# A decoder layer and a gated cross attention: first sums and normalizations in another order, MLP weight pieces over more steps, softmax reciprocal ahead of the smallest values

## The chip, the cores and the metric

The kernel runs on one core of one Trainium2 chip, as one program. The metric is the device time of one execution in microseconds (us). The engines are TensorE (PE; its weight loads are listed apart as PEld), VectorE (DVE), ScalarE (ACT), GpSimd (POOL) and SyncE (SP, which issues most DMAs). Each runs its own instructions in order and waits on semaphores for the others.

## The reference

Everything is float32: `x` is 16 batches of 128 tokens by 512 features, the context `ctx` likewise. There are 16 heads of 32 features.

```python
def layer0(x, ctx):                                 # decoder layer
    ln = layernorm(x, ln1_s, ln1_b)
    q, k, v = split(ln @ w_qkv + b_qkv, 3)
    x = x + merge(attention(q, k, v, mask_SxS)) @ w_ao + b_ao
    ln = layernorm(x, ln2_s, ln2_b)
    q = ln @ w_q + b_q;  k, v = split(ctx @ w_kv + b_kv, 2)
    x = x + merge(attention(q, k, v, mask_BxSxS)) @ w_co + b_co
    ln = layernorm(x, ln3_s, ln3_b)
    return x + gelu(ln @ w1 + b1) @ w2 + b2         # 512 -> 2048 -> 512

def layer1(x, ctx):                                 # gated cross attention
    a = layernorm(ctx, gamma, beta)
    q, k, v = x @ Wq.T, a @ Wk.T, a @ Wv.T
    return x + tanh(gate) * (merge(attention(q, k, v, mask_BxS)) @ Wo.T)

out = layer1(layer0(x, ctx), ctx)
# attention: softmax(q k^T / sqrt(32) * mask - 10000 * (1 - mask)) v, by head
```

## The kernel before

The 16 batches are handled in four groups of four batches (512 tokens). The stages follow each other: self attention of groups A0 to A3, cross attention of B0 to B3, the MLP of the four groups (C0 to C3), and the gated cross attention of D0 to D3. Tiles carry these letters in their names (`s_A`, `ln_C`, `k_D`; a digit for the group is left out in the profile). The token activations `x` stay in SBUF.

The order on each engine is the order in which the program is written down (`keep_in_program_order`). `attend` writes it in steps: a group has 16 steps, four for each batch, and a step handles one unit, which is the scores of a batch for four heads (a 128x512 tile). Unit k goes through the steps as follows: in its own step DVE multiplies the scores out of PSUM by the mask's factor (`scale_unit`) and POOL adds the mask's second term (`add_mask`; the gated stages D have no such addition on POOL); a step later DVE finds each row's smallest value (`least_unit`; the scores are kept with the sign turned, so this is the softmax's maximum) and ACT takes four exponentials with row sums (`exp_unit`); two steps later DVE takes the reciprocal of the sums and POOL multiplies by it (`norm_unit`); three steps later DVE transposes 32x32 squares and SP writes the unit to DRAM (`turn_unit`, tile `away`). SP reads two units back in turned order (`receive_pair`, tile `pT`), PE multiplies by the values (`mix`, tile `av`), and PE multiplies by the output weight (`out_project`, tile `mo`).

Beside the units, each step runs the jobs of the next group (`jobs`: its q, k and v products and what belongs to them) and prepares the group after that (`prepare`: normalizations, which go to DRAM as `turned` and come back as `back`). What must wait for a PE result is put off with `afterwards` and written down when `due()` is called, at a step's start.

The q, k and v products of stage A, and the MLP's products, use block products: a 512x512x512 product becomes seven products of blocks instead of eight, with sums of weight blocks (`left_blocks`, tiles `sums`, made once) and of token blocks (`right_blocks`, tiles `sums_A`, made for each group) before them, and sums out of PSUM after them. One block product is eight matmuls of 128x256. `BLOCKS` gives the steps at which the seven products are issued. Products 1, 6 and 7 add up in one PSUM bank (`mm0`), and ACT copies the bank after each; products 5 and 3 share `mm1`; products 2 and 4 use one of the two banks `pt`.

Before the first group there are no units to run beside. `SelfAttention.begin` normalizes A0 (`normalize`: DVE's statistics, POOL's power for the inverse deviation, then the normalization itself), transposes it on PE, and makes the sums of the q weights; `attend` then runs the jobs of A0 in 16 steps and prepares A1 beside them. In `normalize`, a flat tile is normalized by DVE (`rest`), a tile in squares (all groups after the first) by ACT with an offset from DVE (`rest_in_squares`).

The gated layer's weights must be turned: `gated_weight` loads a weight in 32x32 squares (16 DMAs), DVE transposes it in four parts, and each part is kept in DRAM. In the kernel before this happens to Wk beside the first products, to Wv beside A0's attention (in the jobs of A1), to Wq and Wo in stage B.

The MLP starts beside the last group of stage B. `beside_last_cross` gives its jobs by step, from 0 to 23: key and value products of D0 (`gated_start`), the normalization of C0 (`mlp_start`, whose four reads back, `back_C`, come at step 6), and `piece`, which runs the generator `mlp` on by one `yield`. The first weights `w1_0`, `w1_1` and `w2_0` (1 MB each) are loaded in four pieces each, one piece per `next`:

```python
        while pieces:
            pieces.popleft()()
            yield
```

`piece` calls `due()` first, so that in steps 2 to 13 deferred work is also written down inside the step.

Of the kernel before, what the change touches and what calls it, by code (L numbers as in the profile page):

```python
# [16 lines left out]
P = 128  # L17
# [4 lines left out]
H = 512  # L22
# [30 lines left out]
def decoder_then_gated_cross_attention(ctx: ExitStack, tc: tile.TileContext, a: dict, out: bass.AP):  # L53
# [7 lines left out]


    flip, in_blocks = [0], [True]

    def ps(tag, name):
        if tag == "mm" and in_blocks[0]:
# [151 lines left out]
    def normalize(src, dst, name, then):  # L218

        mv = work.tile([P, 2], F32, tag="mv", name=f"mv_{name}", bufs=4)  # L220
        st = work.tile([P, 6], F32, tag="st", name=f"st_{name}", bufs=4)
        nc.vector.bn_stats(st, src)
        nc.vector.bn_aggr(mv, st)
        rstd = work.tile([P, 1], F32, tag="rstd", name=f"rstd_{name}", bufs=4)
        nc.vector.tensor_scalar(rstd, mv[:, 1:2], EPS, None, ALU.add)
        nc.gpsimd.tensor_tensor(rstd, rstd, mhalf[:, 0:1], ALU.pow)

        def rest():
            nc.vector.tensor_scalar(dst, src, mv[:, 0:1], rstd, ALU.subtract, ALU.mult)
            then()  # L230

        def rest_in_squares():

            off = work.tile([P, 1], F32, tag="off", name=f"off_{name}", bufs=4)
            nc.vector.scalar_tensor_tensor(off, mv[:, 0:1], -1.0, rstd, ALU.mult, ALU.mult)
            nc.scalar.activation(by_chunk(dst), squares(src), AF.Identity, bias=off, scale=rstd)
            afterwards("dve", then)

        afterwards("dve", rest if len(dst.shape) == 2 else rest_in_squares)

    def ln_tile(name):
        return work.tile([P, GB, NQ, KC, Q], F32, tag="ln", name=f"ln_{name}")
# [322 lines left out]
    def attend(sections, ready, others, after=None):  # L565

        if not ready:
            sections[0].begin()
            jobs = sections[0].jobs()
            for p in range(NS):
                due()
                for job in jobs.get(p, ()):
                    job()
                sections[1].prepare(p)
        units, batches = [], []
        projected = deque()  # L580

        def step(k, bt=None, jobs=(), ahead=None, last=True):

            m = k % GB
            pair = k - 5
            if pair % 2 and 0 <= pair < len(units):
                receive_pair(*units[pair])
            if m == 0 and bt is not None:
                scores(bt)
            due()  # L590
            for job in jobs:
                job()
# [12 lines left out]
            if 0 <= k - 3 < len(units):  # L605
                turn_unit(*units[k - 3])
            if 0 <= k - 1 < len(units):
                least_unit(*units[k - 1])
                exp_unit(*units[k - 1])
            if 0 <= k - 2 < len(units):  # L610
                norm_unit(*units[k - 2])
            if bt is not None:
                for j in SCALED[m]:
                    scale_unit(bt, j)
                bt.sec.add_mask(by_head(bt.s[m]), bt.b)

# [29 lines left out]
    class SelfAttention(Section):  # L646
# [16 lines left out]
            elif p >= 12:  # L663
                group_back(self.lnT, self.back, "ln1_s", "ln1_b", [p - 12])

        def begin(self):

            ln = work.tile([P, GB, H], F32, tag="ln", name="ln_A0")
            self.lnT = act_tile("A0")
            tp = []  # L670
            for b in range(GB + 1):
                if b == 1:
                    turn_vectors(0)
                    tp += [ps("sc", f"tp_A0_{k}") for k in range(KC)]
                left = late["dve"].popleft() if b else None
                if b < GB:
                    normalize(x[0][:, b, :], ln[:, b, :], f"A0_{b}", lambda b=b: transpose_batch(tp, ln, b))
                if left is not None:
                    left()
            transposed_out(self.lnT, tp, "ln1_s", "ln1_b")  # L680

            at_ = [wpool.tile([P, GB, 2, HF], F32, tag="w", name=f"sums_{n}") for n in range(2)]
            masks = [work.tile([P, 2, 2, HF], F32, tag="mask", name=f"sums_A{n}", bufs=2) for n in range(2)]
            at_ = [t[:, n] for t in at_ for n in range(GB)] + [masks[1][:, 1]]
            SelfAttention.tokens_at = [masks[0][:, 0], masks[0][:, 1], masks[1][:, 0]]
            SelfAttention.weights = []
            for n, key in enumerate(("sq", "sk", "sv")):
                sides, todo = left_blocks(w[key], at_[3 * n : 3 * n + 3])  # L690
                SelfAttention.weights.append(sides)
                SelfAttention.weight_sums.append(todo)
            for o in SelfAttention.weight_sums[0]:
                nc.vector.tensor_tensor(*o)

        weight_sums = []
        v_bias = "b_qkv", 2 * KC

        def jobs(self):
            g, n, lnT = self.g, self.name, self.lnT  # L700
            qkv_tiles(self)
            sides, todo = right_blocks(lnT, self.tokens_at)
            sums = [lambda o=o: nc.gpsimd.tensor_tensor(*o) for o in todo], [0, 0, 1, 2]
            v = self.v
            products = [
                block_product(halves(self.q), self.weights[0], sides, False, f"q_{n}", ("b_qkv", 0)),
# [7 lines left out]
            if g == 0:  # L714
                others = [o for todo in self.weight_sums[1:] for o in todo]
                rows = [lambda b=b: add_row(0, bo_row, b) for b in range(GB)]
                more = (
                    *small_jobs(), *gated_weight("k", "enc", 7), ([lambda o=o: nc.vector.tensor_tensor(*o) for o in others], [1, 2, 3, 3, 4, 5, 6, 7]),
                    (rows, range(8, 12)),
                )  # L720
            elif g == 1:
                more = ([lambda b=b: load_batch(3, b) for b in range(GB)], [1, 3, 5, 7]), *gated_weight("v", "enc")
            return plan(sums, *blocks_plan(products), *more)

        def scale_mask(self, s, sc, b):
# [25 lines left out]
    class CrossAttention(Section):  # L751
# [32 lines left out]
        def jobs(self):  # L784
# [9 lines left out]
            out += [lambda c=c: project_chunk(self.k, w["ck"], encT, c, f"k_{n}", "b_k", 0) for c in range(KC)]  # L794
            out += [lambda b=b: values_chunk(self.v, w["cv"], encT, b, f"v_{n}", w["bcv"]) for b in range(GB)]
            return plan(
                (out, PRODUCTS), ([lambda: mask_terms(self.ms, self.ma)], [7]), *(gated_weight("qo"[g - 1]) if g in (1, 2) else ()),
                *((late_weights(),) if g == 0 else ())
            )

# [34 lines left out]

    def mlp_start(ml):


        ml.b2 = load_row(a["L0_xattn_b2"], "b2_row")
        ml.db1 = cpool.tile([P, NF], F32, tag="db1", name="db1")  # L840
# [31 lines left out]
    def mlp(ml, last_steps):  # L872
# [12 lines left out]

        kept, unkept, pieces = {}, [], deque()

        def load(n, which):  # L890
            g, i = steps[n]
# [125 lines left out]
        w1, w2, right1, right2 = {}, {}, {}, {}  # L1017

        w1[0], w1[1], w2[0] = load(0, 1), load(1, 1), load(0, 2)
        while pieces:  # L1020
            pieces.popleft()()
            yield

        right1[0], todo, _ = sums(0, 1, "kT", w1.pop(0), nc.gpsimd)
        for do in todo:
# [87 lines left out]
    def gated_weight(key, tag="w", first=0):  # L1113

        t = []

        def begin(c, half):
            if not t:
                t.append(act_tile(f"gw_{key}", "enc") if tag == "enc" else wpool.tile([P, KC, H], F32, tag="w", name=f"gw_{key}"))
            load_turned(t[0], a[f"L1_xattn_W{key}"], c, (2 * half, 2 * half + 1))  # L1120

        def turn(c):
# [1 line left out]
            afterwards("act", lambda: keep_part(f"g{key}", t[0], c))  # L1124

        return (
            ([lambda c=c, half=half: begin(c, half) for c in range(KC) for half in range(2)], range(first, first + 8)),
            ([lambda c=c: turn(c) for c in range(KC)], [8, 10, 12, 14] if first == 0 else [12, 13, 14, 15]),
        )

    class FirstGated:
# [130 lines left out]
    def beside_last_cross():  # L1262
# [2 lines left out]
            due()  # L1265
            next(in_mlp)

        at_ = [*range(2, 14), 8, 10, 12, 14, 15, 15, 16, 16, 17, 18, 19, 19, 20, 21, 21, 22, 23, 23]
        pieces = [piece] * len(at_)
        return plan(*gated_start(first), *mlp_start(ml), (pieces, at_))  # L1270

    def beside_last_gated():
        return plan((deferred, [1, 3, 5, 7, 9, 11, 16, 17, 19]))
# [72 lines left out]
```

## Time and profile before

| | |
|---|---|
| time, median of 3 runs | 1218.19 us (1218.03 to 1218.56) |
| the profiled execution's own time | 1217.82 us |
| span from first to last instruction | 1215.8 us |
| mean granted TensorE clock | 0.989 |
| busy, share of the span: PE | 1170.9 us, 96% |
| DVE | 749.1 us, 62% |
| POOL | 592.1 us, 49% |
| ACT | 585.1 us, 48% |
| HBM | 158.70 MB read, 89.13 MB written, 204 GB/s |
| first scores of A0 on PE | 62.10 us from the span's start |

In a timeline line stand the start and the duration in us, engine, line and operation, then the tiles as written<-read, the shapes and the count; in brackets the idle time of the engine before it and what ended that. Almost every instruction is recorded through one helper, so the line is L49 throughout and the tiles tell them apart. "issue" means that the profile shows no releaser. SPq and ACTq are DMA issues on those queues.

### The profile page before, as it was taken

Reading aid. Unit: us, or ns where it says so; the run is one execution under the profiler, and the core shown is the slowest. Engines: PE = TensorE matmul, PEld = TensorE weight load, DVE = VectorE, ACT = ScalarE, POOL = GpSimd, SP = SyncE. Lnnn points to the kernel's source line nnn. Section 1 sums busy time; section 2 is a strip of 40 time slices with the busy share of each in tenths; the row PEclk is TensorE's granted clock in tenths of the full one; section 3 lists DMA queues with packets and bytes.
Section 4 is the critical chain, followed back from the end, with each engine's and each line's share of the span. In section 5 each row is a group of like instructions: output and inputs, shape, how many; then the busy total and the mean of one; then the engine's idle time right before and its main releaser. Section 6 shows DMA issues by size and latency. Waiting matters only on the chain.

```text
span 1215.8 us, 20222 instructions
## 1 busy us (share of the span) xinstructions
PE 1170.9 (96%) x6707; PEld 775.3 (64%) x6707; DVE 749.1 (62%) x1452; ACT 585.1 (48%) x2042; POOL 592.1 (49%) x547
## 2 busy tenths in 40 slices
PE   5979999999999999988999999999999999999997
PEld 4767777744444444434688888888888754444443
DVE  6587979786777767774755443552432247557673
ACT  2256676766665565565222232232222246768652
POOL 4377868675767665567224433443341133323331
PEclk8999999999999999999999999999999999999999
DMA  5768477898887977797694484486447628676575
GB/s 201 181 168 235 144 195 192 226 258 231 194 229 186 235 215 221 191 254 222 201 352 168 170 296 171 156 250 252 148 160 262 194 81 225 167 211 182 166 226 181
DMA packets 317983, 249.18 MB, mean 205 GB/s; under 512 B 82932, under 2 KB 278200, under 8 KB 313016
## 3 DMA queue, kind: packets, MB, share of 16 engines
q1 hardware_dynamic: 317840, 247.89, 69.4%
q8 instruction: 53, 0.87, 0.3%
q14 instruction: 50, 0.41, 0.1%
q10 hardware_dynamic: 40, 0.01, 0.0%
HBM read 158.70 MB, written 89.13 MB: 204 GB/s over the span
## 4 chain that ended last, share of the span: by engine, by line
PE 74%; POOL 9%; issue 6%; DVE 6%; DMA 3%; ACT 1%; SPq 1%; ACTq 0%; POOLq 0%
PE o L49 14%; PE h L49 14%; PE mm_q_D L49 5%; PE mm_v_B L49 5%; PE mm_k_B L49 5%; PE mm_q_B L49 5%; PE mo_A L49 4%; PE mm_v_D L49 4%; PE mm_k_D L49 3%; PE mo_B L49 3%; PE mm_v_A L49 3%; POOL s_A L49 3%; PE mm_k_A L49 2%; PE mo_D L49 2%; POOL s_B L49 2%
## 5 line engine op out<-in xcount | busy, mean ns | idle before, releaser
L49 POOL TENSOR_TENSOR s_D<-s_D,sum_D 128x512 f32<-128x512 f32 x64 | 66.5, 1039 | 142.7 <-DVE sum_D L49 135.3
L49 ACT ACTIVATE s_B<-s_B,mn_B 128x128 f32<-128x128 f32 x256 | 99.5, 390 | 73.9 <-issue 50.9
L49 DVE TENSOR_TENSOR h<-h,h 128x512 f32<-128x512 f32 x80 | 54.9, 686 | 119.1 <-PE h L49 118.7
L49 ACT ACTIVATE s_A<-s_A,mn_A 128x128 f32<-128x128 f32 x256 | 99.6, 393 | 58.4 <-issue 34.3
L49 ACT ACTIVATE s_D<-s_D,mn_D 128x128 f32<-128x128 f32 x256 | 99.4, 390 | 40.1 <-issue 33.3
L49 ACT ACTIVATE h<-h 128x512 f32<-128x512 f32 x64 | 40.3, 630 | 157.9 <-DVE h L49 153.7
L49 POOL TENSOR_TENSOR s_B<-s_B,sum_B 128x512 f32<-128x512 f32 x64 | 67.3, 1052 | 76.9 <-DVE sum_B L49 66.2
L49 POOL TENSOR_TENSOR s_A<-s_A,sum_A 128x512 f32<-128x512 f32 x64 | 66.6, 1040 | 62.6 <-DVE sum_A L49 60.0
L49 POOL TENSOR_TENSOR s_B<-s_B,mask 128x512 f32<-128x512 f32 x64 | 82.3, 1285 | 0.5 <-DVE s_B L49 0.5
L49 POOL TENSOR_TENSOR s_A<-s_A,ma 128x512 f32<-128x512 f32 x64 | 81.6, 1275 | 0.2 <-DVE s_A L49 0.2
L49 POOL TENSOR_TENSOR sh<-h 128x512 f32<-128x512 f32 x32 | 41.5, 1296 | 53.0 <-ACT h L49 43.3
L49 POOL TENSOR_TENSOR rstd_aD<-rstd_aD,mhalf 128x1 f32<-128x1 f32 x12 | 6.6, 550 | 115.2 <-DVE rstd_aD L49 101.8
L49 PE MATMUL h<-T_C,w 128*128 128x256 f32 x256 | 61.1, 381 | 1.1 <-DVE h L49 1.0
L49 PE MATMUL h<-sx,t 128*128 128x256 f32 x256 | 60.7, 380 | 1.2 <-POOL sx L49 1.2
L49 DVE STREAM_TRANSPOSE s_D<-s_D 128x512 f32<-128x512 f32 x64 | 45.4, 709 | 26.3 <-POOL s_D L49 26.2
L49 PE MATMUL h<-T_C,t 128*128 128x256 f32 x256 | 60.7, 380 | 0.6 <-DVE h L49 0.5
L49 PE MATMUL mo_B<-w_co,mT_B 128*128 128x512 f32 x128 | 59.0, 604 | 2.0 <-ACT mT_B L49 2.0
L49 PE MATMUL mo_D<-w_go,mT_D 128*128 128x512 f32 x128 | 57.9, 601 | 2.8 <-ACT mT_D L49 2.8
L49 PE MATMUL mo_A<-w_ao,mT_A 128*128 128x512 f32 x128 | 59.2, 605 | 1.4 <-ACT mT_A L49 1.4
L49 PE MATMUL o<-w,h 128*128 128x256 f32 x256 | 60.5, 379 | 0.0
L49 PE MATMUL o<-t,h 128*128 128x256 f32 x256 | 60.5, 379 | 0.0
L49 PE MATMUL o<-t,sh 128*128 128x256 f32 x256 | 60.5, 379 | 0.0
(216 smaller groups left out, 2770.9 us busy)
## 6 DMA issues: line engine op xcount, KB each, us to landing
t<-kept SPq DMA_DIRECT2D x24, 1024.0 KB
away_A<-s_A SPq DMA_DIRECT2D x64, 256.0 KB
pT_A<-away_A SPq DMA_DIRECT2D x128, 128.0 KB
away_B<-s_B SPq DMA_DIRECT2D x64, 256.0 KB
pT_B<-away_B SPq DMA_DIRECT2D x128, 128.0 KB
away_D<-s_D SPq DMA_DIRECT2D x64, 256.0 KB
pT_D<-away_D SPq DMA_DIRECT2D x128, 128.0 KB
w<-in_L_xattn_w_dram SPq DMA_DIRECT2D x24, 512.0 KB
```

The lines of the kernel that those rows point to most:

```text
L49: return lambda *args, **kw: self.tc.keep_in_program_order(call(*args, **kw))
```

## The change

It has five parts.

1. Until the first attention steps begin, a tile in squares is normalized by DVE, too (`at_start`). From then on ACT does it, as before.
2. The four sums of the q weights move from DVE to POOL. The four token sums of A0 move from POOL to DVE, and all four are written down at once. The preparation of A1 starts one step sooner: its first batch's statistics stand ahead of A0's last step into `T_A`.
3. The turning of Wk gets a tile of its own (one of the two `v` buffers), with loads at steps 4 to 11 instead of 7 to 14. The turning of Wv moves from the jobs of A1 to those of A2, that is from beside A0 to beside A1.
4. In each attention step, `norm_unit` (reciprocal and POOL's product of unit k-2) is written down ahead of `least_unit` and `exp_unit` (of unit k-1).
5. The MLP's first weights come in 12 pieces at steps 1, 3, 4, 5, 8 to 13, 15 and 16 instead of 2 to 13, as jobs of their own that don't call `due()`.

```diff
 def normalize(src, dst, name, then):
...
         def rest():
-            nc.vector.tensor_scalar(dst, src, mv[:, 0:1], rstd, ALU.subtract, ALU.mult)
+            to, of = (by_chunk(dst), squares(src)) if len(dst.shape) == 4 else (dst, src)
+            nc.vector.tensor_scalar(to, of, mv[:, 0:1], rstd, ALU.subtract, ALU.mult)
             then()
...
-        afterwards("dve", rest if len(dst.shape) == 2 else rest_in_squares)
+        afterwards("dve", rest if at_start[0] else rest_by_act)

 attend:
         if not ready:
-            sections[0].begin()
+            sections[0].begin(sections[1])
...
-                sections[1].prepare(p)
+                if p + 1 < NS:
+                    sections[1].prepare(p + 1)
+        at_start[0] = False
...
                 turn_unit(*units[k - 3])
+            if 0 <= k - 2 < len(units):
+                norm_unit(*units[k - 2])
             if 0 <= k - 1 < len(units):
                 least_unit(*units[k - 1])
                 exp_unit(*units[k - 1])
-            if 0 <= k - 2 < len(units):
-                norm_unit(*units[k - 2])

 SelfAttention.begin:
-            transposed_out(self.lnT, tp, "ln1_s", "ln1_b")
...
             for o in SelfAttention.weight_sums[0]:
-                nc.vector.tensor_tensor(*o)
+                nc.gpsimd.tensor_tensor(*o)
+            following.prepare(0)
+            transposed_out(self.lnT, tp, "ln1_s", "ln1_b")

 SelfAttention.jobs:
+            if g == 0:
+                gw_k = work.tile([P, GB, H], F32, tag="v", name="gw_k", bufs=2)
...
+            if g == 0:
+                sums = [], []
+                for o in todo:
+                    nc.vector.tensor_tensor(*o)
...
-                    *small_jobs(), *gated_weight("k", "enc", 7), (others, [1, 2, 3, 3, 4, 5, 6, 7]),
-                    (rows, range(8, 12)),
+                    *small_jobs(), *gated_weight("k", gw_k, range(4, 12), range(12, 16)), (rows, range(8, 12)),
+                    (others, [1, 2, 3, 3, 4, 5, 6, 7]),
             elif g == 1:
-                more = load_batch(3, ...), *gated_weight("v", "enc")
+                more = [load_batch(3, ...)]
+            elif g == 2:
+                more = gated_weight("v", act_tile("gw_v", "enc"))

 mlp:
-        while pieces:
-            pieces.popleft()()
-            yield
+        yield

 beside_last_cross:
-        at_ = [*range(2, 14), 8, 10, 12, 14, 15, 15, 16, 16, 17, 18, 19, 19, 20, 21, 21, 22, 23, 23]
-        pieces = [piece] * len(at_)
-        return plan(*gated_start(first), *mlp_start(ml), (pieces, at_))
+        at_ = [0, 8, 10, 12, 14, 15, 15, 16, 16, 17, 18, 19, 19, 20, 21, 21, 22, 23, 23]
+        loads = [1, 3, 4, 5, 8, 9, 10, 11, 12, 13, 15, 16]
+        return plan(
+            *gated_start(first), *mlp_start(ml), ([piece] * len(at_), at_),
+            ([lambda: ml.pieces.popleft()()] * len(loads), loads),
+        )
```

PE's instructions and their order are the same in both kernels.

More of the change, by code (lines that the diff above doesn't have):

```diff
@@ L63, in decoder_then_gated_cross_attention @@
     flip, in_blocks = [0], [True]
+    at_start = [True]
     def ps(tag, name):
@@ L228, in rest, with rest_by_act @@
         def rest():
[L229 removed]
+            to, of = (by_chunk(dst), squares(src)) if len(dst.shape) == 4 else (dst, src)
+            nc.vector.tensor_scalar(to, of, mv[:, 0:1], rstd, ALU.subtract, ALU.mult)
             then()
[L232 removed]
+        def rest_by_act():
             off = work.tile([P, 1], F32, tag="off", name=f"off_{name}", bufs=4)
@@ L664, in prepare, with begin @@
                 group_back(self.lnT, self.back, "ln1_s", "ln1_b", [p - 12])
-        def begin(self):
+        def begin(self, following):
             ln = work.tile([P, GB, H], F32, tag="ln", name="ln_A0")
@@ L717, in jobs @@
                 more = (
-                    *small_jobs(), *gated_weight("k", "enc", 7), ([lambda o=o: nc.vector.tensor_tensor(*o) for o in others], [1, 2, 3, 3, 4, 5, 6, 7]),
-                    (rows, range(8, 12)),
+                    *small_jobs(), *gated_weight("k", gw_k, range(4, 12), range(12, 16)), (rows, range(8, 12)),
+                    ([lambda o=o: nc.vector.tensor_tensor(*o) for o in others], [1, 2, 3, 3, 4, 5, 6, 7]),
                 )
             elif g == 1:
-                more = ([lambda b=b: load_batch(3, b) for b in range(GB)], [1, 3, 5, 7]), *gated_weight("v", "enc")
+                more = [([lambda b=b: load_batch(3, b) for b in range(GB)], [1, 3, 5, 7])]
+            elif g == 2:
+                more = gated_weight("v", act_tile("gw_v", "enc"))
             return plan(sums, *blocks_plan(products), *more)
@@ L796, in jobs @@
             return plan(
-                (out, PRODUCTS), ([lambda: mask_terms(self.ms, self.ma)], [7]), *(gated_weight("qo"[g - 1]) if g in (1, 2) else ()),
+                (out, PRODUCTS), ([lambda: mask_terms(self.ms, self.ma)], [7]),
+                *(gated_weight("qo"[g - 1]) if g in (1, 2) else ()),
                 *((late_weights(),) if g == 0 else ())
@@ L836, in mlp_start @@
     def mlp_start(ml):
+        ml.pieces = deque()
         ml.b2 = load_row(a["L0_xattn_b2"], "b2_row")
@@ L884, in sums_of @@
             return token_sums(quarters, s3, s2, s4)
-        kept, unkept, pieces = {}, [], deque()
+        kept, unkept, pieces = {}, [], ml.pieces
         def load(n, which):
@@ L1111, in fetch_weight, with gated_weight @@
         w[key] = fetch(key, wpool.tile([P, KC, H], F32, tag="w", name=f"w_{key}"))
-    def gated_weight(key, tag="w", first=0):
-        t = []
+    def gated_weight(key, tile_=None, loads=range(8), turns=range(8, 16, 2)):
+        t = [] if tile_ is None else [tile_]
         def begin(c, half):
             if not t:
-                t.append(act_tile(f"gw_{key}", "enc") if tag == "enc" else wpool.tile([P, KC, H], F32, tag="w", name=f"gw_{key}"))
+                t.append(wpool.tile([P, KC, H], F32, tag="w", name=f"gw_{key}"))
             load_turned(t[0], a[f"L1_xattn_W{key}"], c, (2 * half, 2 * half + 1))
@@ L1126, in gated_weight @@
         return (
-            ([lambda c=c, half=half: begin(c, half) for c in range(KC) for half in range(2)], range(first, first + 8)),
-            ([lambda c=c: turn(c) for c in range(KC)], [8, 10, 12, 14] if first == 0 else [12, 13, 14, 15]),
+            ([lambda c=c, half=half: begin(c, half) for c in range(KC) for half in range(2)], loads),
+            ([lambda c=c: turn(c) for c in range(KC)], turns),
         )
```

## The prediction

> **What bounds the kernel now.** I read the page's busy shares first (PE 96%), then the stretches of busy time by stage, then PE's list of waits, and last the timeline around the longest waits. The change can only win where PE idles or runs at half clock. Columns of the stretches: stretch, its length, then busy us and (instructions) of PE, PEld, DVE, ACT and POOL, granted clock, DMA share, GB/s.
>
> ```profile
> 12.00:22.00 10.00, 5.88 (x17) 4.57 (x18) 8.82 (x13) 2.01 (x4) 5.64 (x5) 1.00 0.60 214
> 22.00:31.00 9.00, 7.98 (x24) 6.08 (x24) 5.05 (x9) 2.49 (x5) 3.57 (x4) 0.62 0.23 66
> 60.00:100.00 40.00, 33.77 (x236) 27.80 (x238) 34.11 (x68) 22.90 (x89) 31.41 (x30) 0.91 0.75 194
> ...
> 535.00:540.00 5.00, 5.00 (x13) 2.26 (x12) 3.38 (x7) 2.62 (x14) 4.00 (x4) 1.00 1.06 237
> 540.00:545.00 5.00, 1.62 (x7) 0.35 (x6) 3.99 (x8) 3.69 (x15) 3.16 (x3) 1.00 0.91 277
> 545.00:550.00 5.00, 2.19 (x29) 1.83 (x30) 2.58 (x5) 0.96 (x6) 4.05 (x5) 0.51 0.91 260
> ...
> 1050.00:1100.00 50.00, 50.00 (x350) 24.40 (x349) 30.72 (x64) 37.71 (x148) 16.47 (x16) 1.00 0.73 205
> ```
>
> Three places lose time, and the change works at all three: the first products (12 to 31 us: 5.1 us idle, then clock 0.62), the first attention group A0 (60 to 100: 6.2 idle, clock 0.91), and the group beside the MLP's start (540 to 550: 6.2 idle, then clock 0.51, while the DMA engines were full). From 250 to 500 and 1000 to 1140 PE is full; there the change can only lose.
>
> At the start PE waits 4.12 us, because ACT's queue is in order: ACT must normalize a batch of the next group before it may copy the first product's bank, and that normalization waits for DVE's offset.
>
> ```profile
> 18.81 1.21 DVE L49 SCALAR_TENSOR_TENSOR off_A<-mv_A,rstd_A 128x1 f32<-128x1 f32 x1 [0.66 <-POOL rstd_A L49]
> ...
> 20.11 0.81 ACT L49 ACTIVATE ln_A<-x,off_A,rstd_A 128x512 f32<-128x512 f32 x1 [7.63 <-issue]
> 20.82 0.82 ACT L49 ACTIVATE q_A<-mm_q_A,vcols 128x256 f32<-128x256 f32 x2
> 21.74 2.66 PE L49 MATMUL mm_q_A<-sums_A,sums 128*128 128x256 f32 x8 [4.12 <-issue]
> ```
>
> In A0, DVE's row of one step shows the softmax order: smallest value, then reciprocal, then POOL's scaling; POOL sits idle 0.95 us for it.
>
> ```profile
> 73.76 0.69 DVE L49 TENSOR_REDUCE mn_A<-s_A 128x4 f32<-128x512 f32 x1 [0.52 <-POOL s_A L49]
> 74.37 0.17 DVE L49 RECIPROCAL sum_A<-sum_A 128x4 f32<-128x4 f32 x1
> 74.68 1.04 POOL L49 TENSOR_TENSOR s_A<-s_A,sum_A 128x512 f32<-128x512 f32 x1 [0.95 <-DVE sum_A L49]
> 87.08 1.45 PE L49 MATMUL sc_A<-k_A,q_A 32*128 32x128 f32 x26 [3.33 <-DVE s_A L49]
> ```
>
> Beside the MLP's start one write-out of probabilities is issued at 536.89, behind four reads back (back_C, 1 MB) and two weight pieces; the read that waits for it begins at 543.63, and PE's value product at 547.81.
>
> ```profile
> 536.89 0.38 SPq L49 DMA_DIRECT2D away_B<-s_B  x1
> 543.63 1.74 SPq L49 DMA_DIRECT2D pT_B<-away_B  x4
> 547.81 1.92 PE L49 MATMUL av_B<-pT_B,v_B 128*32 128x128 f32 x28 [6.19 <-DMA pT_B<-away_B]
> ```
>
> **The change, part by part.** PE's order is the same in both programs, so each part is a matter of when its operands are there.
>
> *Start.* ACT loses four normalizations of 0.81 and DVE four offsets; DVE gains four normalizations (0.54, the row of ln_A at 9.91) and the four token sums (0.69); POOL takes the four sums of w_sq (1.27 each) in place of the token sums. New delay: POOL's sums now begin at 9.9, just when DVE needs its last normalization of the first group. Two-input sums on POOL and DVE exclude each other in the trace (DVE's sum at 14.04 took 1.64 and ended 0.54 after POOL's), and DVE's small mask product at 41.79 took 1.19 beside POOL's. So I let that normalization wait for one POOL sum, 1.1 us, and the first product begins at 13.0 instead of 11.86. DVE's statistics of x1 stand before T_A too; 2.36 MB must have landed, which the packets of before reach by about 9.5, before DVE asks at 11.6. From there PE has 21 products up to the first scores: the first two took 5.77 (x16, slow clock), the other 19 take 1.73 each in the chain, 32.9; and it waits 0.9 at each of two bank copies (ACT's 0.84 row), 0.8 for DVE at the k/v bank, 0.9 for the small transposes and the scores: 3.4. That is 42.1, and the first scores stand at 55.1 instead of 62.10: **7.0 us less**. What hides the added DVE work: DVE must finish the add out of bank mm1 (c22 of q) before PE reaches the product after it, at 27.9. Counted from T_A's end at 14.2: four token sums up to 17.8 (each waiting for one of POOL's), normalization and transpose 1.3, one sum of w_sk 1.1, statistics 1.1, add 0.65, again 1.3, three sums 2.4, statistics 1.1, add 0.65: 27.4. So the cover is half a microsecond thin; with it gone, every DVE collision (about 1.1) is PE's. I take 7.0, between 4 (three collisions more) and 8.5 (no lock at 9.9, one bank wait hidden). The gated key weight's loads start three steps sooner, in another buffer; the 0.92 that DVE waited for them at 60.43 goes into the same sum. SP passes them in front of w_ao and the small vectors, each issue about 0.45, whose users come over 5 us later.
>
> *A0.* With the reciprocal first, POOL scales right after the mask. Going through the rows from 69.9 to 87: scaling at 73.74 instead of 74.68, the next at 77.85 instead of 78.64, then 80.1 instead of 81.86, but DVE, full from 81 on, brings the last scale forward by only 0.8. So the 3.33 wait becomes 2.5 and the 1.88 behind it about 1.4: 1.3 in all. The half clock from 87.72 to 94.54 costs 2.1 (PE had 4.1 us of work in it); a shorter wait may avoid it, which I count as 1.2. **2.5 less**, between 0 and 5. The gated value weight's 16 loads, 4 stores and 4 transposes (0.70) move from A0 to A1, to the same steps, where PE is full: 0, at worst 1 us lost there.
>
> The clock term is where a rule must be weighed. In this trace the waits of 4.12, 3.33 and 6.19 were each followed by 6.83 us at half clock, those of 1.98 and 2.10 by none, so the limit lies between 2.1 and 3.3, and my two remaining waits (2.5 and 2.9) stand inside: hence part of the gain. The Trainium skill ("TensorE: Matmul & The Clock Gate", section "Why this matters for your kernels") says that gaps over about 3 us drop the clock; by it alone both half-clock terms would go whole, 4.1 instead of 2.4.
>
> *MLP weights.* The 12 pieces (256 KB each) go from steps 2 to 13 to steps 1, 3, 4, 5, 8 to 13, 15, 16: none beside back_C. The pieces also no longer flush deferred work inside their step, so back_C is issued in two halves a step apart and ACT's key and value copies come after the exponentials of the step. Ahead of the late write-out, from the write of the unit two earlier on, stand 2.25 MB instead of 2.75; at 237 GB/s that is 2.1 us, and it is issued about 1 us sooner (two back_C issues and a piece, 0.45 each): 3.2 of the 6.19 go. The half clock cost 0.84 on the value product (1.92 against 1.08) and 1.11 on mm_v_D (4.81 against 3.70); I count 1.2 of it. **4.5 less**, between 1 and 7. What is late next: the last w2 pieces come at steps 15 and 16 instead of 13, and DVE's sums of w2 at 573.61 would wait for the last (issue about 571, some 2.5 to land): up to 1 us, in the lower bound.
>
> *Reciprocal first, elsewhere.* The smallest value of unit k-1 now queues behind a reciprocal that waits for ACT's exponentials of unit k-2, and ACT waits for the smallest value: 0.08 plus 0.77 (572.95 to 573.03, 572.35 to 573.12). In the full stages PE covers it; at the end the step was 2.5 (POOL's norms at 1188.49, 1191.00) and becomes 1.58 of exponentials plus 0.88: 0, within 1 us.
>
> Sum: 7.0 + 2.5 + 4.5 = 14.0. The profiled execution took 1217.82 for a span of 1215.8; the median of the runs is 0.37 above it, 1218.19. Forecast 1218.19 - 14.0 = 1204.2.
>
> **Rivals.** *DVE becomes the start's bound* (0.16): it was busy 8.82 of 10 us there already and takes on more. Then the start gives 3 and the time is 1208. Against it: ACT no longer stands between. *The write-out stays late* (0.14): the DMA engines are full over 525 to 560, whatever the order; then the last term falls to 0.5, 1208. Both together: 1212. *Slower* (0.07): in the gated stages nothing on POOL gates the smallest value, so it ran ahead; now it can't. ACT's busy time per step of 4.06 is 3.06 (37.71 of 50), and with 0.94 uncovered (0.77 plus the reciprocal's 0.17) it is 4.00: 0.06 short of the step. If ACT's waits for products add 0.35 to that, 0.29 over 64 steps is 18.6, and the time 1223; it decides from 0.28, where the 14 are eaten (14 / 64 + 0.06). Against it: ACT's copies lie between the two exponentials and hide most. *Nothing moves on the chip* (0.03): the new waits eat the gains, 1218.
>
> **How the numbers follow.** The forecast's own case (0.60) spans 1199 to 1208. To leave out 2 in 10 I take in the two partial cases and their sum: 1197 to 1212, the low end all three terms near their upper bounds. Faster by over 0.2% (2.4 us, about what can be told from no change) 0.90, same 0.03, slower 0.07.
>
> **What would show it.** The first sc_A at 54 to 57 instead of 62.10, no half clock around 23 to 30, ACT's q_A copy right behind the first product; POOL's 0.95 idle before its scaling gone in A0; the wait of av_B for pT_B at 2 to 4 instead of 6.19. Wrong would be: sc_A later than 59, a new PE wait for ACT exponentials between 1000 and 1140, or av_B's wait unchanged.

## The result, and the profile after

The changed kernel takes 1208.18 us (median of 6 runs, 1206.61 to 1210.17), the kernel before 1218.38 beside it (6 runs, 1216.34 to 1218.93). The ratio is 0.9918, 95% interval 0.9906 to 0.9931: faster by 10.0 us, with an interval of 8.4 to 11.5. The profiled execution took 1208.67 for a span of 1206.7, 0.5 above the median; its span is 9.1 shorter than that of before. The forecast was 1204.2: right in direction and inside its range, and 4 too hopeful.

PE's order is the same in both programs, so the gain can be read as a lead: how much sooner the same batch of scores begins on PE. It is 5.48 at A0's first scores (62.10 to 56.62), 8.56 at the end of A3 and all through B0 to B2, 13.60 at the last scores of B3 (554.40 to 540.80), 10.20 at the first scores of D0, and 9.03 at the last scores of D3. So the start and B3 gave most, and B3 took 3.4 back shortly after.

The stretches of the changed kernel, with the columns as in the prediction:

```profile
12.00:22.00 10.00, 8.84 (x32) 6.85 (x32) 9.67 (x17) 2.94 (x6) 6.21 (x7) 1.00 0.65 225
22.00:31.00 9.00, 9.00 (x43) 7.93 (x42) 8.68 (x16) 1.68 (x4) 2.92 (x3) 1.00 0.23 67
60.00:100.00 40.00, 35.80 (x251) 28.97 (x250) 33.47 (x69) 28.40 (x115) 34.35 (x33) 0.91 0.66 181
...
540.00:545.00 5.00, 5.00 (x42) 2.46 (x41) 1.21 (x2) 3.63 (x11) 3.00 (x3) 1.00 0.93 272
560.00:565.00 5.00, 1.86 (x26) 1.19 (x29) 0.00 (x0) 0.95 (x4) 1.82 (x2) 1.00 0.84 242
565.00:570.00 5.00, 5.00 (x33) 3.96 (x25) 4.91 (x8) 0.58 (x1) 1.39 (x1) 0.66 0.52 144
1050.00:1100.00 50.00, 49.67 (x334) 24.00 (x323) 30.41 (x62) 37.00 (x144) 16.02 (x16) 1.00 0.71 195
```

At the start PE went from 5.88 to 8.84 of 10 us, and the half clock of 22 to 31 (0.62) is gone. 60 to 100 won 2.0 of busy PE at the same clock of 0.91. 540 to 545 is full, where PE stood for 3.4. But 560 to 570 now looks as 540 to 550 did, on a smaller scale: 3.1 idle, then clock 0.66. In the D stretch 0.33 is idle where nothing was.

Timeline of the changed kernel around the start: ACT, DVE and PE.

```profile
16.26 0.84 ACT L49 ACTIVATE q_A<-mm_q_A,vcols 128x256 f32<-128x256 f32 x2 [3.00 <-PE mm_q_A L49]
19.72 0.84 ACT L49 ACTIVATE q_A<-mm_q_A,vcols 128x256 f32<-128x256 f32 x2 [2.62 <-PE mm_q_A L49]
...
9.77 1.48 DVE L49 TENSOR_SCALAR ln_A<-x,mv_A,rstd_A 128x512 f32<-128x512 f32 x1 [0.44 <-POOL rstd_A L49]
26.05 0.69 DVE L49 TENSOR_TENSOR q_A<-mm_q_A,q_A 128x512 f32<-128x512 f32 x1
...
17.79 1.89 PE L49 MATMUL mm_q_A<-sums_A,sums 128*128 128x256 f32 x8
20.61 1.99 PE L49 MATMUL mm_q_A<-T_A,sums 128*128 128x256 f32 x8 [0.93 <-ACT q_A L49]
42.77 0.23 PE L49 MATMUL tv<-ident,vrows 48*128 48x48 f32 x1 [1.70 <-DMA vrows<-in_L_xattn_ln_beta_dram]
```

ACT copies each bank as soon as PE has filled it. The product that waited 4.12 (at 21.74 before) now follows at 17.79 without a wait; the next one waits 0.93, where before had 1.02. DVE's add at 26.05 ends before the product after it (27.62), with 0.9 to spare. What is new is the last line: 1.70 for a small vector's load.

SP's issues, changed kernel:

```profile
31.82 0.49 SPq L49 DMA_DIRECT2D w_ao<-in_L_xattn_w_ao_dram  x1
32.35 1.03 SPq L49 DMA_DIRECT2D gw_k<-in_L_xattn_Wk_dram  x2
33.48 0.77 SPq L49 DMA_DIRECT2D turned_A<-ln_A  x1
...
36.14 0.32 SPq L49 DMA_DIRECT2D vrows<-in_L_xattn_b_kv_dram  x1
38.69 0.87 SPq L49 DMA_DIRECT2D gw_k<-in_L_xattn_Wk_dram  x2
39.60 0.38 SPq L49 DMA_DIRECT2D vrows<-in_L_xattn_ln_s_dram  x1
```

Between 36.46 and 38.69 SP issues nothing. The DMA queue's list of waits names the reason, a line that before does not have:

```profile
SPq L49 <- DMA w_ao<-in_L_xattn_w_ao_dram: 2.2, 1, 2.2
```

The issue at 38.69 is the eighth after that of w_ao (two of gw_k, turned_A, four vrows, then this one), and by this list it waited until w_ao, 1 MB, had landed (median 6.9 us from issue to landing). The line stands in all seven profiles that have the changed start and the vectors behind w_ao, with 1.9 to 3.2 us. Before, SP waited 5.8 us for DVE's ln_A right after it had issued w_ao, and issued nothing behind the load meanwhile. That it is the eighth issue is counted here and was not tested: with the vectors moved (below) no wait for w_ao is listed, though one issue of gw_k there takes 3.01. The last five vectors are issued behind it, 1.7 later than before (41.08 against 39.36), and their user comes 5.4 sooner than in before, its wait included.

In A0 POOL scales without the idle 0.95 (74.46 directly follows 73.20 + 1.26), and the wait of the scores is 2.32 instead of 3.33:

```profile
74.14 0.18 DVE L49 RECIPROCAL sum_A<-sum_A 128x4 f32<-128x4 f32 x1 [0.16 <-ACT s_A L49]
74.46 1.04 POOL L49 TENSOR_TENSOR s_A<-s_A,sum_A 128x512 f32<-128x512 f32 x1
74.50 0.69 DVE L49 TENSOR_REDUCE mn_A<-s_A 128x4 f32<-128x512 f32 x1 [0.18 <-POOL s_A L49]
80.57 1.88 PE L49 MATMUL sc_A<-k_A,q_A 32*128 32x128 f32 x26 [2.32 <-DVE s_A L49]
```

Beside the MLP's start, the value product that waited 6.19 waits 1.97; the last but one now waits 3.14, and DVE waits for the last piece of w2:

```profile
534.53 1.79 PE L49 MATMUL av_B<-pT_B,v_B 128*32 128x128 f32 x28 [1.97 <-DMA pT_B<-away_B]
556.59 0.71 DVE L49 STREAM_TRANSPOSE s_B<-s_B 128x512 f32<-128x512 f32 x1 [2.89 <-POOL s_B L49]
564.56 1.13 PE L49 MATMUL av_B<-pT_B,v_B 128*32 128x128 f32 x28 [3.14 <-DMA pT_B<-away_B]
565.09 0.69 DVE L49 TENSOR_TENSOR t<-w,t 128x512 f32<-128x512 f32 x1 [5.39 <-DMA w<-in_L_xattn_w_dram]
```

### The profile page after: what moved, and what is told of

It is laid out like the page before. It is cut to its first block, busy times and chain, and to the rows that moved or that the text cites. A ratio compares the mean times of both kernels' runs of the same rounds, so it can differ in the third digit from the quotient of the medians.

```text
span 1206.7 us, 20209 instructions
## 1 busy us (share of the span) xinstructions
PE 1169.3 (97%) x6707; PEld 774.5 (64%) x6707; DVE 749.4 (62%) x1452; ACT 580.8 (48%) x2038; POOL 594.2 (49%) x547
## 5 line engine op out<-in xcount | busy, mean ns | idle before, releaser
L49 PE MATMUL mm_q_D<-T_D,w_gq 128*128 128x512 f32 x128 | 59.4, 613 | 0.0
```

The lines of the kernel that those rows point to most:

```text
L49: return lambda *args, **kw: self.tc.keep_in_program_order(call(*args, **kw))
```

## The experiments

Times are compared by each kernel's ratio to the kernel before, run beside it on the same chip. One kernel's executions spread over 1 to 9 us (the last section shows where much of it comes from), so single profiles are read for where a wait stands, and for the size of a lead only where several agree.

**The three parts alone.** First the start (with the moves of the gated weights), the changed kernel with this undone:

```diff
-            norm_unit(k - 2); least_unit(k - 1); exp_unit(k - 1)
+            least_unit(k - 1); exp_unit(k - 1); norm_unit(k - 2)
...
-        loads = [1, 3, 4, 5, 8, 9, 10, 11, 12, 13, 15, 16]
+        at_ = [*range(2, 14), ...]      # one piece per next(in_mlp), as before
```

> The changed kernel with the old softmax order (smallest value first) and the old placing of the MLP's pieces; only the start's edits and the moves of the two gated weights stay. My theory is that the parts act each in its own place: first scores at 56.6 as in the changed kernel (62.10 before), this lead of 5.5 kept unchanged through A0 to A3 (the further 3.1 won there belong to the softmax order), av_B's wait for pT_B again about 6.2, and 1218.2 - 5.5 = 1212.7 at the end. Rival: what was won in A0 to A3 comes from the gated value weight's 16 loads having left A0; then the lead grows to 7 to 8.6 by the end of A3 and the time is about 1210.

Measured 1213.22, ratio 0.9961 (0.9949 to 0.9973): 4.7 faster than before. First scores at 56.88, the lead 5.22 there and 5.15 at the end of A3; av_B waits 7.3 again. At the first scores of A0, three profiles with the old start have 61.01, 62.10 and 63.14 and the six with the whole changed start and the vectors unmoved 56.27 to 56.88 and once 60.54: means 62.1 and 57.2, 4.8 apart, as the ratio says. So the start acts by itself, and what A0 to A3 gained beyond it does not come from the gated value weight's jobs.

Next the order alone, in the kernel before:

```diff
-            least_unit(k - 1); exp_unit(k - 1); norm_unit(k - 2)
+            norm_unit(k - 2); least_unit(k - 1); exp_unit(k - 1)
```

> The kernel before with one edit: the reciprocal and scaling of a unit stand ahead of the next unit's smallest value. My theory: first scores unchanged at 62.1, a lead of 1.5 by the end of A0 and of 3.1 by the end of A3, the wait for pT_B beside the MLP's start still 5 to 6.2, and 1.2 lost in the last gated sections (scores waiting for DVE's scaling): 1218.2 - 3.1 + 1.2 = 1216.3. Rival: the order wins nothing by itself, because the gated value weight's jobs are still in A0: then 1219.4. The slower rival of the prediction (ACT short of time in the gated stages) would show as more than 1.2 lost from 1000 to 1140.

Measured 1219.08, ratio 1.0001 (0.9983 to 1.0019). The profile has a lead of 1.1 at the first scores, where nothing was changed, then the order's gain in A0 to A3 (the lead grows by 2.4) and the two losses in D (1.2), but beside the MLP's start it lost 2.7 more: av_B waits 6.8, mo_B 3.7, and half clock follows both. The forecast of 1216.3 for it was too good; within about 2.2 us either way, the order is worth nothing in this kernel. Half clock has a part in that: over its ten executions the mean granted clock is 0.987, over those of the kernel before 0.989, which makes 2.7 us (an estimate: 0.0022 of 1218).

Then the pieces alone, in the kernel before:

```diff
-        at_ = [*range(2, 14), ...]; pieces = [piece] * len(at_)
+        loads = [1, 3, 4, 5, 8, 9, 10, 11, 12, 13, 15, 16]
+        ..., ([lambda: ml.pieces.popleft()()] * len(loads), loads)
```

> The kernel before with one edit: the twelve pieces of the MLP's first weights at steps 1, 3, 4, 5, 8 to 13, 15 and 16, no longer flushing deferred work. My theory: nothing moves before 530; av_B's wait for pT_B falls from 6.19 to about 3, a lead of 5 to 6 at the last scores of that section, of which DVE's wait for the last piece of w2 takes 3.5 to 4.3 back: a lead of 1.5 to 2.5, 1216.2. Rival: the shorter wait came from the softmax order, which issues the write-out sooner; then av_B's wait stays near 6, DVE still waits for the last piece, and the time is 1218 or above.

Measured 1213.24, ratio 0.9958 (0.9945 to 0.9971): 5.1 faster, 3 better than I expected. In its profile the wait of 6.19 is 1.53 without the new order, so the pieces did it. It holds over all profiles: from 500 to 600 PE idles 11.7 to 12.9 in the three with the old pieces, 7.6 to 11.2 in the eleven with the spread ones, means 12.1 and 9.1. The three ratios add up to the whole: 0.39% + 0.42% - 0.01% = 0.80%, against 0.82%.

**What takes the lead back beside the MLP's start.** My first theory was DVE's wait of 5.39 for the last piece of w2.

```diff
-        loads = [1, 3, 4, 5, 8, 9, 10, 11, 12, 13, 15, 16]
+        loads = [1, 3, 4, 5, 8, 9, 10, 11, 12, 13, 15, 15]
```

> The changed kernel with the last piece of w2 at step 15 instead of 16, so that SP no longer issues it behind the four reads pT_B that wait for the write-out. My theory: DVE's wait of 5.39 for that piece goes (below 1.5) and PE's loss behind it of 3.4 to 4.3 with it, half clock after it included: 1208.2 - 3.4 = 1204.8. Rival: 256 KB more in front of the write-out make av_B's wait for pT_B longer by 1.1 (256 KB at 237 GB/s) or more and another wait takes the place: 1207 to 1208.5.

Measured 1209.56, ratio 0.9931 (0.9916 to 0.9947). DVE's wait fell as it should, and PE's did not. Timeline of this kernel, DVE and PE:

```profile
562.84 0.99 DVE L49 TENSOR_TENSOR t<-w,t 128x512 f32<-128x512 f32 x1 [1.69 <-DMA w<-in_L_xattn_w_dram]
565.84 1.07 PE L49 MATMUL av_B<-pT_B,v_B 128*32 128x128 f32 x28 [2.86 <-DMA pT_B<-away_B]
```

The moved piece has a price (the wait of 1.97 is 2.54 here), but that lies ahead of the last scores of B3. Behind them 3.3 of the lead are lost, as in the changed kernel (3.4). So that theory falls: the longest new wait in the list was harmless, and the 3.14 on PE does not hang on it. The second theory was POOL's queue (the 2.89 at 556.59 above).

```diff
-        return ..., [lambda o=o: nc.gpsimd.tensor_tensor(*o) for o in operands]
+        return ..., [lambda o=o: eng.tensor_tensor(*o) for o in operands]   # first group: nc.vector
```

> The changed kernel with the four sums of the MLP's first tokens on DVE instead of POOL. The last run spoke against my first theory of what took back 3.4 to 4.3 of the lead beside the MLP's start (DVE's wait of 5.39 for the last piece of w2): with that wait at 1.69 the time stayed. New theory: POOL's queue sets the tail there; DVE's transpose at 556.59 waited 2.89 for a scaling that stood behind two token sums of 1.27, and PE then waited 3.14 for pT_B, with half clock after it. With the sums on DVE the scaling comes 2.5 sooner, the wait of av_B falls below 1, and the lead at 580 becomes 12.5 or more instead of 10.2: 1205.5. Rival: the DMA queue sets it (the read pT_B itself takes 4.8 from issue to use); then av_B still waits about 3 and the time is 1208.

Measured 1208.09, ratio 0.9931 (0.9908 to 0.9954): no gain. The transpose came 2.8 sooner (553.79) and av_B's wait fell, but another took its place, so that 3.14 became 4.17. Timeline of this kernel, PE:

```profile
561.72 0.41 PE L49 MATMUL av_B<-pT_B,v_B 128*32 128x128 f32 x4 [2.18 <-ACT h L49]
564.12 1.21 PE L49 MATMUL av_B<-pT_B,v_B 128*32 128x128 f32 x28 [1.99 <-DMA pT_B<-away_B]
```

What all profiles with the spread pieces share (11, with the runs below) is a longer time from the last scores of B3 to their last two value products. Timeline of the kernel before, PE:

```profile
554.40 1.17 PE L49 MATMUL sc_B<-k_B,q_B 32*128 32x128 f32 x32
575.54 1.28 PE L49 MATMUL av_B<-pT_B,v_B 128*32 128x128 f32 x32
594.26 1.08 PE L49 MATMUL av_B<-pT_B,v_B 128*32 128x128 f32 x32
```

It is 21.1 and 39.9 us here, and 23.0 to 25.5 and 41.6 to 44.3 with the spread pieces. With the order alone it is 23.3 and 41.1, so the pieces are not the only cause. Nor is it a limit that only a large lead runs into: from the last scores of B3 to the first of D0 the pieces alone lose 3.7 of a lead of 5.9, and the four kernels with sooner vectors (below) 1.8 to 3.8 of 14.6 to 17.6. I read it that what follows the last scores (softmax of the last four units, write-out, read back) takes some 2 to 4 us longer, whatever the lead. Which link of that chain ends last stays open; taking away either of the two that I suspected did not help.

**The order, taken out of the changed kernel,** in the gated stages only:

```diff
-            norm_unit(k - 2); least_unit(k - 1); exp_unit(k - 1)
+            if not ready: norm_unit(k - 2)
+            least_unit(k - 1); exp_unit(k - 1)
+            if ready: norm_unit(k - 2)                  # ready: the gated stages
```

> The changed kernel with the reciprocal and scaling ahead of the smallest value only in the decoder's eight sections; in the gated sections D the old order is back. My theory: the two losses of 0.58 near 1050 and 1102, where the scores wait for DVE's scaling, are gone, nothing else moves, and the time is 1208.2 - 1.2 = 1207.0. Rival: those losses come from the earlier arrival of the whole stage, whatever its order; then they stay, 1208.2.

Measured 1207.50, ratio 0.9913 (0.9885 to 0.9940). The losses in D are gone. This holds over all profiles: PE idles 0.7 from 1010 to 1140 in each of the six with the new order in D and 0.0 in each of the eight with the old one. In the changed kernel the place is this (timeline, DVE and PE):

```profile
1037.21 0.18 DVE L49 RECIPROCAL sum_D<-sum_D 128x4 f32<-128x4 f32 x1 [0.47 <-ACT s_D L49]
1040.39 0.68 DVE L49 TENSOR_TENSOR s_D<-sc_D,gma 128x512 f32<-128x512 f32 x1
1041.13 1.15 PE L49 MATMUL sc_D<-k_D,q_D 32*128 32x128 f32 x26 [0.33 <-DVE s_D L49]
```

DVE's reciprocal waits for ACT's exponentials; the smallest value and the scaling out of PSUM queue behind it, and the next scores wait 0.33 for their bank. The time itself is not told apart from the changed kernel's.

And everywhere, from the changed kernel:

```diff
-            norm_unit(k - 2); least_unit(k - 1); exp_unit(k - 1)
+            least_unit(k - 1); exp_unit(k - 1); norm_unit(k - 2)
```

> The changed kernel with the old softmax order everywhere: the start and the pieces alone. The order alone changed nothing in the time (ratio 1.0001): it won 2.4 in A0 to A3, and 3.6 was lost beside the MLP's start and in D. My theory: with the spread pieces the gain of A0 to A3 would also be capped beside the MLP's start, so without the order the lead is 5.5 at the first scores and at 500, about 9 at 580, and D loses nothing: 1208.2 to 1209. Rival: the order's gain does survive beside the spread pieces; then the lead at 580 is 7 and the time 1211.

Measured 1206.24, ratio 0.9910 (0.9885 to 0.9934): the same as the changed kernel. Without the order the lead is 5.8 at the first scores and 5.4 at the end of A3 (8.56 with it), yet at the first scores of D0 it is 10.3 (10.2 with it). In D it then grows to 12.1 where it falls to 9.0 with the order: 1.2 of that is the order's loss in D, and 1.7 is half clock behind the first scores of D0, which this profile happens not to have (last section). In this pair of profiles the lead of the order is lost again beside the MLP's start.

**The start.** ACT normalizes again:

```diff
-        afterwards("dve", rest if at_start[0] else rest_by_act)
+        afterwards("dve", rest if len(dst.shape) == 2 else rest_by_act)
```

> The changed kernel with the start's normalizations of the next groups on ACT again, with their offsets on DVE; the start's sums stay where the change puts them. My theory: ACT's place between two bank copies is what made PE wait 4.12 at the start, so at least 3 of the 5.5 won are lost: first scores at 60 to 62, with a wait over 2 us at the third product of q. Rival: the 5.5 come from the other start edits (the sums on the two engines, the next group prepared a step sooner); then first scores at 56.6 or, with DVE relieved of 0.54 four times, sooner.

Measured 1210.87, ratio 0.9941 (0.9924 to 0.9958), 2.8 slower than the changed kernel; the intervals touch, and the waits are what shows the cause. First scores at 60.16, so 3.5 of the 5.5 are ACT's place; the other 2.0 come from the rest of the start. Against the kernel with the vectors moved (54.74, below) ACT's place is worth 5.4: in the changed kernel the wait for the vectors hides part of it. PE waits again for a bank behind a normalization (timeline of this kernel, PE; another wait, of 2.37, stands at 19.67):

```profile
24.20 2.72 PE L49 MATMUL mm_q_A<-T_A,sums 128*128 128x256 f32 x8 [2.56 <-ACT q_A L49]
```

The small vectors ahead of the gated weight and of w_ao:

```diff
-            [5, 4, 6, 7, 8, 10, 10, 11],
+            [5, 4, 2, 3, 8, 10, 10, 11],
```

> The changed kernel with the two jobs that load the small vectors of the second kind at steps 2 and 3 instead of 6 and 7, so that they stand ahead of the 1 MB load of w_ao and of the gated key weight's loads on SP's queue. My theory: PE's wait of 1.70 (2.5 in the kernel without the new order) for the last of those vectors goes, first scores at 54.9 instead of 56.6, and that lead is kept up to the group beside the MLP's start, which keeps half of it or more: 1206.5 to 1207.4. Rival: the 0.45 us issues now delay the weight loads ahead of them and the first products wait for those; then first scores at 56.6 or later, 1208.2 or above.

Measured 1204.30, ratio 0.9891 (0.9866 to 0.9917). That is 2 to 3 us better than I expected, and by the ratios 3.3 below the changed kernel, of which the first scores explain 1.9. First scores at 54.74, and the product that waited 1.70 waits for no load (timeline of this kernel, PE):

```profile
40.85 0.26 PE L49 MATMUL tv<-ident,vrows 48*128 48x48 f32 x1
```

**Together.** The sooner vectors with the old order everywhere, with the new order in the decoder only, and the latter with the token sums on DVE (each the diffs above, joined):

> The changed kernel with the small vectors' loads at steps 2 and 3 and the old softmax order everywhere. The order's gain in A0 to A3 (3.1) was taken back beside the MLP's start and in D in every profile so far. Theory: the order is worth nothing on balance, so this is as fast as the sooner vectors with the new order or faster by the 1.2 of D: 1203 to 1205. Rival: with the start sped up further the order's gain survives, and this kernel is 2 or more slower than the vectors alone: 1206 or above.

> The changed kernel with the small vectors' loads at steps 2 and 3, and the new softmax order in the decoder's sections only. Theory: the 1.7 to 3.9 of the vectors (a wait of 2.65 for them was followed by products at half clock in one profile) and the 1.2 of D add up: 1204.3 - 1.2 = 1203.1. Rival: they do not add, 1204.3 or above.

> The kernel with the sooner vectors and the new order in the decoder only, and the four first token sums of the MLP on DVE. Alone, these sums on DVE brought av_B's last wait from 3.14 to 1.99 and put 2.2 for ACT's copy of h in its place. Theory: nothing is won by them here either, within 1 us of the kernel without them: 1203. Rival: with a lead that is larger POOL's queue limits the tail more, and 2 us are won: 1201.

Measured 1206.65, ratio 0.9907 (0.9895 to 0.9920); 1205.02, 0.9894 (0.9880 to 0.9908); 1204.78, 0.9892 (0.9876 to 0.9909). First scores at 54.73, 55.47 and 54.94. The third is no better than the second: the token sums win nothing, as expected. By the numbers that I put down for the first, its rival came out (1206 or above: the order's gain survives). The 1.2 of D did not show in the time beside the vectors (1205.0, not the 1203.1 that I expected), and whether the order pays in the decoder alone is not settled: in this pair of profiles its lead did last (14.73 in D with it, 12.52 without), but the intervals of the first two overlap. The three kernels with sooner vectors that keep the order in the decoder have 0.9891 to 0.9894 against the changed kernel's 0.9918, some 3 us below it; each of their intervals still overlaps its interval, so this is likely rather than shown.

## Why the prediction was right or wrong

*Start, forecast 7.0, measured 5.5 in the profile and 4.7 by the ratio of the start alone.* The mechanism held, and nearly to the row: in the profile of the changed kernel DVE's normalization at 9.77 took 1.48 beside POOL's sum, the first product came at 12.65 (forecast 13.0), DVE's add ended at 26.7 (27.4), 0.9 ahead of the product that needs it (forecast 0.5). In five of the eleven profiles with the sums on these engines the normalization took 0.55 and the first product came at 11.5 to 12.1; in three of these PE then waits 0.1 to 0.5 up to the end of DVE's add, so the cover is as thin as I said. The step that failed is the sentence that SP passes the gated key weight's loads "in front of w_ao and the small vectors, each issue about 0.45, whose users come over 5 us later". I priced the issues and not a queue that stops: 2.2 for w_ao, and the user, moved up 7.1 by the rest of the start (48.21 to 41.07), waited 1.70. With the vectors moved, the first scores stand at 54.73 to 55.47 in four kernels; the forecast was 55.1. That it fits so closely has luck in it: in the changed kernel the first two products took 5.1 and not 5.77, and the small items about as much more than I had counted (the four waits that I listed add up to 3.5, not 3.4).

*A0, forecast 2.5, measured 1.55 in the profile and nothing in the time.* The wait fell from 3.33 to 2.32 (forecast 2.5), but half clock still followed it (80.75 to 87.57), so the 1.2 for the clock was wrong. The rule behind it, a limit between waits of 2.1 and 3.3, already had a row against it in the kernel before: its wait of 1.43 at the first scores of D0 is followed by 3.4 us at half clock (988.84 to 992.25). A1 to A3, which I had put at nothing, gave another 1.5. The lead was there and the time does not show it: three comparisons with and without the order in A0 to A3 gave ratios that can't be told apart.

*MLP weights, forecast 4.5, measured 5.1 by the ratio of the pieces alone.* The wait of 6.19 became 1.97 (3.0 forecast; 1.53 alone). In the changed kernel the lead grew by 5.0 to the last scores and 3.4 were lost behind them. I had named a loss there, "up to 1 us", with the wrong cause: the last w2 piece. So the profile of the changed kernel keeps only 1.6 of this part at the first scores of D0 (10.2 against 8.56), and that without the order 4.9 (10.3 against 5.4): beside the MLP's start it is the order's lead that is lost, in this pair. (The terms listed for this part add up to 4.4, not 4.5.)

*gw_v to A1, forecast 0:* with this move and without the order the lead stays level (5.22 to 5.15), as forecast. *Reciprocal first elsewhere, forecast 0 within 1:* -1.2, the mild form of the slower rival. Its mechanism is there, ACT's exponentials in front of DVE's queue, but it cost 0.58 of lead in two places (a wait of 0.33 in each), and not 0.28 in each of 64 steps. That rival's sum used the wrong step: 4.06 is a step of stage B (16.24 from one batch's scores to the next), while in D the scores come every 12.81, a step of 3.20. With it ACT's 2.41 and the 0.94 make 3.35, 0.15 too long and some 10 us over 64 steps (an estimate from these rows); that it cost 1.2 fits the counter-argument, that ACT's copies hide most. So the forecast of about nothing here was right for a reason that its sum did not give.

The sum: 14.0 forecast, 10.0 measured; by the ratios 2.3 of the difference lies in the start and 2.5 in the order, while the pieces gave 0.6 more. Of the rivals, "DVE becomes the start's bound" is out: DVE was busy 9.67 of 10 us and still on time, or late by half a microsecond at most. "The write-out stays late" is out, too: the wait of 6.19 fell to 1.97, and to 1.53 with the pieces alone.

## What to carry to other kernels

When loads are moved ahead on a queue, count the issues behind every large one: here the eighth issue after a 1 MB load stood still until that load had landed, and small loads behind it paid. A lead in an early stage need not last: the start's came through to the end, the order's in two of three pairs of profiles did not. So sum the parts by runs of each part alone, not by the leads that one profile shows. The longest new wait of a trace need not cost anything; remove it and see.

## What the runs showed of the hardware

The half clock is not decided by the length of a wait as I had assumed. At the first scores of D0 PE waits 1.42 or 1.43 in every kernel; in 6 of the 14 profiles the next 24 products then took 12.26, at half clock for about 3.4 us, and in 8 they took 10.57. A wait of 2.32 (A0 here) was followed by 6.83 us at half clock, waits of 1.70 and 2.46 for the vectors by none, and one of 2.65 for them by products of 3.78 instead of 1.99. The Trainium skill's limit of about 3 us ("TensorE: Matmul & The Clock Gate", section "Why this matters for your kernels") does not tell these apart; in these runs a wait of 1.4 can be enough, and 2.5 need not be.

The granted clock, read in slices of 0.25 us over three parts of every profile (17 to 110, 482 to 610 and 952 to 1010 us), shows more. Every stretch at half clock there lasts 3.41, 6.83 or 10.24 us, and within a profile all of them begin on one grid with steps of 3.413 us. In the kernel before they begin at 22.86, 87.72, 545.11 and 988.84, which are 19, 134 and 130 steps apart. The grid lies differently from profile to profile, also where the start of the kernels is the same. Cut along it, the same traces give 46 steps at full clock that a step at half clock follows. PE idled at least 1.42 in each of them, and every step at full clock with 1.96 or more of idle is among them; in between there are both kinds. Six of the steps:

| profile | step, us | PE idle in it | clock in the next step |
|---|---|---|---|
| changed kernel, A0 | 77.33 to 80.75 | 2.32 | 0.50 |
| new order in the decoder only, vectors | 39.67 to 43.09 | 2.10 | 0.50 |
| changed kernel, vectors | 39.79 to 43.20 | 1.70 | 1.00 |
| start alone, vectors | 38.80 to 42.21 | 1.65 | 1.00 |
| before, D0 | 985.42 to 988.84 | 1.43 | 0.50 |
| sooner vectors, D0 | 971.39 to 974.80 | 1.42 | 1.00 |

So the wait of 2.46 (start alone) was harmless because a border of the grid cut it into 1.65 and 0.81. The two rows of D0 have the same idle time; they differ in how much of the score products (32 rows) lies in the step, 1.49 to 1.65 us in the six profiles with half clock and 0.98 to 1.48 in the eight without. That these products count as partly idle is a guess from this and was not tested.

So a pair of profiles can differ by 1.7 us at D0 alone, with the same wait there. Half clock is also behind much of the spread of one kernel's executions: of the ten of the order alone, the fastest (1212.98) has a mean granted clock of 0.992 and the slowest (1222.41) of 0.983.
